# A four-layer graph network on one Trainium2 core: the end of the nearest-neighbour search, the bias, the third pass's row order and the attention loop's first loads are moved

## The chip, the cores and the metric

One core of a Trainium2 chip (trn2) runs the whole kernel. The metric is the device time of one execution in microseconds (us), as the median of several runs, lower is better. The profile shows one execution by its engines: PE (TensorE; PEld is its weight load), DVE (VectorE), ACT (ScalarE), POOL (GpSimd) and SP (SyncE). A name such as SPq is an engine's queue of DMA issues.

## The reference, cut to what matters

The inputs are `x` (2708 nodes of 128 features) and the dense matrix `adj` A (2708 x 2708, f32). Four layers follow each other, each `x = layernorm(x + layer(x))`. Only the first two touch the change:

```python
# layer 0
d  = 1/sqrt(rowsum(A));  z = leaky_relu(d*(A @ (d*x)) @ W1 + b1, 0.1)
S  = exp(-sqrt(max(|z_i - z_j|^2, 0) + 1e-10) / 2), kept for the 4 nearest j of each i
d2 = 1/sqrt(rowsum(A + S))
x  = layernorm(x + d2*((A + S) @ (d2*x)) @ W2 + b2)
# layer 1
XW  = x @ W;  s_col = XW @ a[:128];  s_row = XW @ a[128:]
den = exp(leaky_relu(s_row[:,None] + s_col[None,:], 0.01));  num = A @ den
x   = layernorm(x + A @ ((den/num) @ XW))
# layers 2 and 3: a normalised and a plain product with A, each with a linear map
```

## The kernel before

**Tiles.** The 2708 nodes are T = 22 tiles of 128 rows: 21 full ones and a last one of 20. The 2708 columns are C = 6 chunks (four of 512, one of 384, one of 276), each of three or four tiles. `adjT` holds A transposed in HBM. The tile `ring` takes its strips as they are loaded; `res` keeps the last RES = 6 tiles of rows.

**Stages in order of time.** The first product with A and the projection to `z` end at about 155 us. The search (L699 to L702) then takes one tile of nodes at a time: twelve matmuls give the negated distances, ACT copies them to `key`, and DVE finds the eight largest (`max`, L701) and their places (`max_index`, L702). The order of the tiles is 4 to 15, 0 to 3, 16 to 20; tile 21 was done early. `weigh` turns the four nearest of some tiles into weights (`sim`), the degrees into `d2inv`, and `x` into `y2 = d2inv * x`, which is written to HBM as `y_rows`. It is called for tiles 0 to 16 after tile 16, for 17 to 19 after tile 19, and for 20 and 21 after the search. Inside it, `others` finds which neighbour is the node itself and sorts out the other three. Its steps are on POOL, except for tiles 20 and 21, where DVE does them.

The second pass (L204, `by_panels`) is A times `y2`, chunk by chunk. Meanwhile POOL gathers three neighbours for each tile from `y_rows` (`gather_near`, L729), and DVE sums them with their weights (`sum_near`, L738 and L742). PE, DVE and ACT run in an order written by hand here: an object `Due` counts one tick per row tile of the product, and `at(n, f)` runs `f` at tick n. `near_at[t]` is the tick of `sum_near(t)`. A chunk is closed by `end_pass2`: its neighbour sums are added on PE (`add_near`, L749) at tick `max(due.n + 1, near_at[last tile] + 3, ended[-1] + 16)`, followed by the layer's linear map (L780), the bias and the norm (`norm0`), a transposition (L798) and the comparisons that rank all nodes. The bias `b2` is added to all of `xs` at once (`add_bias`, L265), before the pass.

The third pass (`turns`, L1337) sums weighted rows of A to make the carries of the attention loop. A `line` is half a row tile of A, loaded by SP into one of eleven berths in `ring`, `more` and `y_place` (`load_line`, L1035). As soon as PE has read a berth, the next line that uses it is loaded. An `own_line` is half a tile of `res` and needs no load. `turns` is the order, written by hand, in which PE takes lines, the ranking matmuls (`in_rank_order`, `counts`, `ranks_known`, `in_list_order`) and the weights of the loop (`next_weights`). `end_half(h)` copies the sums of half h out of PSUM and sends them into the tile `carry` by four DMAs on ACT's queue (L1363).

Then comes a branch (`tc.If`, L1773) on a flag which all engines read (L1512), and behind it the attention loop of 44 steps, `block_layer`. In step i, `load(i)` brings the rows by two gathers on POOL (L1498) and two small DMAs on SP (L1505, from `carry`); PE makes `num` (L1619) in a wide and a narrow piece; ACT inverts it (L1452, L1455); DVE corrects and scales it (L1462, L1466, L1469); `keep` saves two rows of the error into `carry` (L1634, four DMAs on SP); and PE adds the product up (L1477). Each step is loaded two steps ahead, into one of three strips of `ring`. The loop's first ACT instruction is the load of a function table (L1609). Layers 2 and 3 follow from about 730 us on.

Every DMA that SP and ACT issue takes the next of eight completion semaphores and waits until the DMA eight before it has ended.

Of the kernel before, what the change touches and what calls it, by code (L numbers as in the profile page):

```python
# [13 lines left out]
ALU = mybir.AluOpType  # L14
# [38 lines left out]
def kernel(  # L53
# [310 lines left out]
    with tc.tile_pool(name="knn", bufs=1) as knn:  # L364
# [225 lines left out]

        def weigh(ts):

            t0, t1 = ts[0], ts[-1] + 1
            nr, sm = near[:, t0:t1, :TOPK], sim[:, t0:t1, :]

            nc.vector.tensor_add(nr, nr, nsq[:, t0:t1, None].to_broadcast([P, t1 - t0, TOPK]))
            nc.vector.tensor_scalar(nr, nr, 0.0, DIST_EPS, op0=ALU.min, op1=ALU.subtract)
            nc.scalar.activation(sm, nr, AF.Ln, scale=-1.0)
            nc.scalar.activation(sm, sm, AF.Exp, scale=0.5)
            nc.scalar.activation(sm, sm, AF.Exp, scale=-0.5)  # L600
            dd = d2inv[:, t0:t1]
            nc.vector.tensor_reduce(dd, sm, AX.X, ALU.add)
            nc.vector.tensor_add(dd, dd, deg[:, t0:t1])  # L603
            nc.scalar.activation(dd, dd, AF.Ln)
            nc.scalar.activation(dd, dd, AF.Exp, scale=-0.5)
            if t1 < T:
                nc.gpsimd.tensor_mul(
                    y2[:, t0:t1, :], xs[:, t0:t1, :], d2inv[:, t0:t1, None].to_broadcast([P, t1 - t0, D])
                )
            else:  # L610
                scale_rows(y2, xs, d2inv, ts)
                spread(y2[:, FULL, :])
# [5 lines left out]
            if full < t1:  # L618
                queue.dma_start(y2_rows[FULL * P :, :], y2[:LAST, FULL, :])
            else:  # L620
                for a in range(t0, t1, 11):
                    others(range(a, min(a + 11, t1)), nc.gpsimd)

# [48 lines left out]
        ready = [load_panel(g, 0) for g in range(G)]  # L672
        tc.keep_in_program_order(nc.scalar.preload_act_table_set("natural_log_exp_and_others"))
        with tc.tile_pool(name="keys", bufs=3) as keys:

            for n, t in enumerate([*range(4, S), *range(4), *range(S, FULL)]):
# [18 lines left out]
                for c in range(C) if n else (5, 3, 2, 4, 1, 0):  # L695
                    if not n:
                        norms(c)
                    cs = cols[c]
                    nc.tensor.matmul(pks[c][:p, : cw[c]], lhsT=z2[:, :p], rhs=zT[:, cs], start=False, stop=True)  # L699
                    nc.scalar.copy(key[:p, cs], pks[c][:p, : cw[c]])  # L700
                nc.vector.max(near[:p, t, :], key[:p])  # L701
                nc.vector.max_index(where[:p, t, :], near[:p, t, :], key[:p])  # L702
                if t == T - 6:
                    weigh(range(0, T - 5))
                if t == T - 3:
                    weigh(range(T - 5, T - 2))
            weigh(range(T - 2, T))
            others(range(T - 2, T), nc.vector)

    psum.close()  # L710
# [62 lines left out]
    nc.vector.memset(rows_d, 0.0)  # L773
    add_bias(b2_sb)
    rk = rk_pool.tile([P, T], F32, tag="rk", name="rk")
# [181 lines left out]
    at = due.at  # L957
    near_at = [24 + (23 * t) // 5 for t in range(T)]
    for t in range(T):
        at(near_at[t], sum_near, t)  # L960
    at(20, nc.vector.memset, rk_f, float(OOB))

# [66 lines left out]
    def line_at(n):  # L1029

        return berths[stays[n]]
# [15 lines left out]
    def fetch_xw(xws, q):  # L1047
# [3 lines left out]
            oob_is_err=False,  # L1051
        )

    with tc.tile_pool(name="rank", bufs=1) as rank:
# [296 lines left out]

        HEADS = 96

        def end_half(h):
# [4 lines left out]
            nc.scalar.copy(tot[:, : edges[4] - edges[3]], banks[h][:, : edges[4] - edges[3]])  # L1359
            nc.scalar.copy(tot[:64, edges[4] - edges[3] :], banks[h][:64, edges[4] - edges[3] : span])  # L1360
            for g in range(4):
                w = edges[g + 1] - edges[g]
                nc.scalar.dma_start(  # L1363
                    carries[0][HEADS : HEADS + 2 * NCH, h * HALF + edges[g] : h * HALF + edges[g + 1]],
                    tot[32 * g : 32 * g + 2 * NCH, :w],
                )
# [45 lines left out]
        def line(n):  # L1412
            for _ in range(n):
                at = loaded[0]
                loaded[0] += 1
                i, h = lines[at]
                add_line(i, h, line_at(at), last=at == 2 * S - 1)
                if at in follows:
                    load_line(follows[at])

        def own_line(n):
            for _ in range(n):
                h, i = divmod(held[0], FULL - S)
                held[0] += 1
                add_line(S + i, h, res[:, i, h * HALF : (h + 1) * HALF], last=held[0] == FULL - S)
                if held[0] == FULL - S:
                    end_half(0)

        turns = [
            (line, 4), (blocks_of_edges,), (line, 7), (own_line, 2), (last_xw,), (in_rank_order, 0), (line, 2),  # L1430
            (in_rank_order, 1), (line, 2), (in_rank_order, 2), (count_lone,), (line, 2), (counts,), (line, 1),
            (add_last_rows, 0), (own_line, 3), (line, 2), (ranks_known,), (line, 1), (own_line, 1), (in_list_order, 0),
            (line, 1), (in_list_order, 1), (in_list_order, 2), (line, 1), (own_line, 1), (in_list_order, 3),
            (line, 1), (add_last_rows, 1), (next_weights,), (own_line, 1), (next_weights,), (line, 1), (next_weights,),
            (own_line, 1), (next_weights,), (line, 1), (next_weights,), (own_line, 1), (line, 1), (next_weights,),
            (line, 5),
        ]
        for f, *args in turns:
            f(*args)
        for c in range(C):  # L1440
            nc.sync.dma_start(res[few(c), FULL - S, cols[c]], adjT[FULL * P :, cols[c]])
        end_half(1)
        carry = carries[0]
        assert loaded[0] == 2 * S and held[0] == 2 * (FULL - S) and work["groups"] == 6
        xws, lw = work["xws"], work["lw"]
        order.close()
    more.close()
# [33 lines left out]
    psum.close()  # L1481
    adj_half = adjT.rearrange("n (h k) -> (n h) k", h=2)
    WIDE = 2 * CW
    NARROW = HALF - WIDE
    assert 0 < NARROW <= CW

    def block(s):

        return s % NCH * CH + s // NCH

    steps = [(h, q) for h in range(2) for q in range(NQ)]
    rows = {}

    def load(i):
        h, q = steps[i]
        rows[i] = strip(i).rearrange("p (n k) -> p n k", n=2)
        for n in range(2):
            nc.gpsimd.indirect_dma_start(  # L1498
                out=rows[i][:KC, n, :], out_offset=None, in_=adj_half[:, :],
                in_offset=bass.IndirectOffsetOnAxis(ap=slot_i[h][:KC, 2 * q + n : 2 * q + n + 1], axis=0),  # L1500
                bounds_check=2 * N - 1, oob_is_err=False,
            )
            b = block(2 * q + n)
            at = 2 * b if b % CH else HEADS + b // CH * 2
            nc.sync.dma_start(rows[i][KC : KC + 2, n, :], carry[at : at + 2, h * HALF : (h + 1) * HALF])  # L1505

# [97 lines left out]
    def block_layer():  # L1604
        with (
# [40 lines left out]
            with tc.manual_schedule(engines={e.engine for e in engines}):  # L1646
                load(0)
                load(1)
                late_q = list(range(SOON, NQ))
# [165 lines left out]
```

## Time and profile before

| what | us |
|---|---|
| median of three runs | 1066.23 (1063.72 to 1070.17) |
| the profiled execution, its own time | 1063.12 |
| its span, first to last instruction | 1061.4 |
| PE busy | 984.6 (93%) |
| DVE / ACT / POOL busy | 637.0 / 331.5 / 275.1 |
| search, last matmul ends | 286.9 |
| second pass, first matmul | 287.46 |
| third pass, first line | 442.42 |
| third pass, last line ends | 499.04 |
| loop, first `num` / first `hacc` | 502.04 / 512.60 |

In a timeline row the columns are start, duration, engine, line, operation, tiles and shapes, count, and in brackets the idle time of that engine just before it and what ended it. A waits row gives who waited for whom: total us, times, longest. A windows row gives the length of a stretch, the busy time of PE, PEld, DVE, ACT and POOL (with counts), the granted PE clock (1.00 is full speed), the busy share of the DMA engines and GB/s. A busy PE is not a PE at its peak: a matmul at half clock is busy for longer.

### The profile page before, as it was taken

What the parts mean: (1) busy time and instruction counts of PE and PEld (TensorE: products, weight loads), DVE (VectorE), ACT (ScalarE), POOL (GpSimd) and SP (SyncE); (2) the same over time, 40 slices, a digit from 0 to 9 for tenths busy, and PEclk for the clock granted to TensorE, in tenths of its full rate; (3) what the DMA queues carried; (4) which work ended last, traced back from release to release, by engine and by line L of the source; (5) the groups of instructions that cost most, each with busy time, mean ns of one, the idle gap of its engine ahead of it and who ended that gap; (6) DMA issues with size and microseconds to landing.
All of it is one profiled execution on the core that took longest, in us unless ns stands there. A gap on an engine that the chain in (4) does not pass through costs nothing.

```text
span 1061.4 us, 11655 instructions
## 1 busy us (share of the span) xinstructions
PE 984.6 (93%) x3773; PEld 482.9 (45%) x3773; DVE 637.0 (60%) x1358; ACT 331.5 (31%) x609; POOL 275.1 (26%) x339
## 2 busy tenths in 40 slices
PE   0898999999998998796899999999999999999996
PEld 0346544444444556562333333334445544564444
DVE  5985438999944577862899999994121121222222
ACT  0000126555501245402767776762010100010000
POOL 4000000000477673023788534430121100000000
PEclk9989999999998998698999999999999999999998
DMA  9999340000185666696455555556665957484652
GB/s 339 373 342 270 109 157 1 0 1 1 32 279 183 221 182 201 224 359 200 118 167 152 149 146 157 142 163 215 219 193 169 308 168 219 145 276 149 227 170 72
DMA packets 102001, 191.00 MB, mean 180 GB/s; under 512 B 14022, under 2 KB 43342, under 8 KB 101930
## 3 DMA queue, kind: packets, MB, share of 16 engines
q1 hardware_dynamic: 83764, 152.22, 43.5%
q0 software_dynamic: 17728, 37.62, 12.8%
q8 instruction: 32, 0.52, 0.2%
q10 hardware_dynamic: 438, 0.31, 0.1%
q14 instruction: 39, 0.32, 0.1%
HBM read 214.80 MB, written 4.16 MB: 206 GB/s over the span
## 4 chain that ended last, share of the span: by engine, by line
PE 48%; DMA 1%; DVE 1%; ACT 1%; issue 1%; POOL 0%; POOLq 0%; DVEq 0%
PE acc L204 28%; PE num L1619 9%; PE hacc L1477 9%; PE mis L285 1%; DMA ring<-carry 1%; DMA ring<-in_adjT,slot_i 0%; PE mis L1750 0%; DVE inv L1466 0%; DVE err L1462 0%; ACT gb L234 0%; PE mis L1716 0%; DVE inv L1469 0%; PE mis L1746 0%; ACT inv L1452 0%; POOL rstd L253 0%
## 5 line engine op out<-in xcount | busy, mean ns | idle before, releaser
L1498 POOL DMA_INDIRECT ring<-in_adjT,slot_i x88 | 104.4, 1187 | 95.9 <-PE num L1619 67.0
L1619 PE MATMUL num<-ring,lw 128*64 128x512 f32 (+1 forms) x528 | 113.7, 557 | 6.1 <-DMA ring<-carry 3.8
L1477 PE MATMUL hacc<-inv,xws 128*128 128x512 f32 (+1 forms) x264 | 111.7, 559 | 0.6 <-ACT inv L1455 0.3
L699 PE MATMUL acc<-zT,z 128*128 128x512 f32 (+2 forms) x252 | 102.2, 552 | 0.0
L1452 ACT ACTIVATE inv<-num,plain 128x1024 f32<-128x1024 f32 x88 | 80.6, 916 | 57.6 <-PE num L1619 41.4
L253 POOL TENSOR_TENSOR rstd<-rstd,minus_half 128x4 f32<-128x4 f32 (+1 forms) x18 | 17.3, 960 | 313.5 <-DVE rstd L252 313.5
L234 ACT COPY gb<-acc 128x512 f32<-128x512 f32 (+2 forms) x18 | 9.6, 535 | 251.1 <-PE acc L204 251.1
L1462 DVE TENSOR_TENSOR err<-inv,num 128x1024 f32<-128x1024 f32 x88 | 74.6, 856 | 21.0 <-ACT inv L1455 19.7
L700 ACT COPY key<-acc 128x512 f32<-128x512 f32 (+2 forms) x126 | 67.1, 535 | 55.1 <-issue 27.9
L204 PE MATMUL acc<-ring,y 128*128 128x512 f32 (+2 forms) x192 | 82.0, 558 | 0.5 <-issue 0.5
L1477 PEld LDWEIGHTS hacc<-inv,xws 128*128 128x128 f32 x264 | 46.5, 189 | 77.6 <-issue 34.2
L729 POOL DMA_INDIRECT got<-y_rows,where x66 | 71.5, 1083 | 26.6 <-DVE near_sum L742 8.9
L204 PE MATMUL acc<-ring,xs 128*128 128x512 f32 (+2 forms) x192 | 78.1, 550 | 0.0
L1469 DVE SCALAR_TENSOR_TENSOR inv<-gb,g_inv,inv 128x1024 f32<-128x1024 f32 x88 | 77.2, 917 | 0.1
L204 PE MATMUL acc<-ring,carry 128*128 128x512 f32 (+2 forms) x192 | 74.5, 542 | 0.0
L204 PE MATMUL acc<-ring,m_rows 128*128 128x512 f32 (+2 forms) x192 | 74.3, 542 | 0.0
L1466 DVE SCALAR_TENSOR_TENSOR inv<-err,inv 128x1024 f32<-128x1024 f32 x88 | 72.3, 861 | 0.1
L575 POOL TENSOR_TENSOR slot_e<-near,sim 128x44 f32<-128x44 f32 (+2 forms) x3 | 0.7, 241 | 267.3 <-DVE d2inv L603 265.2
L699 PEld LDWEIGHTS acc<-zT,z 128*128 128x128 f32 x252 | 45.8, 190 | 50.4 <-issue 45.0
L1455 ACT ACTIVATE inv<-inv 128x1024 f32<-128x1024 f32 x88 | 67.6, 768 | 2.8
L1619 PEld LDWEIGHTS num<-ring,lw 128*64 128x64 f32 x528 | 37.4, 138 | 65.0 <-issue 47.5
L701 DVE MAX8 near<-key 128x8 f32<-128x2708 f32 x21 | 62.3, 2965 | 2.7 <-ACT key L700 2.7
(376 smaller groups left out, 1370.0 us busy)
## 6 DMA issues: line engine op xcount, KB each, us to landing
ring<-in_adjT SPq DMA_DIRECT2D x74, 1024.0 KB
ring<-in_adjT SPq DMA_DIRECT2D x20, 677.0 KB
ring<-in_adjT SPq DMA_DIRECT2D x17, 768.0 KB
part<-in_adjT SPq DMA_DIRECT2D x12, 1024.0 KB
ring<-in_adjT SPq DMA_DIRECT2D x17, 552.0 KB
more<-in_adjT SPq DMA_DIRECT2D x10, 677.0 KB
res<-in_adjT SPq DMA_DIRECT2D x4, 1280.0 KB
part<-in_adjT SPq DMA_DIRECT2D x3, 768.0 KB
```

Of the source, the lines that this page charges most:

```text
L204: nc.tensor.matmul(accs[c][: lhsT.shape[-1], :w], lhsT=lhsT, rhs=src, start=start, stop=stop)
L699: nc.tensor.matmul(pks[c][:p, : cw[c]], lhsT=z2[:, :p], rhs=zT[:, cs], start=False, stop=True)
L700: nc.scalar.copy(key[:p, cs], pks[c][:p, : cw[c]])
L729: nc.gpsimd.indirect_dma_start(out=got[:p, :], out_offset=None, in_=y2_rows[:, :], in_offset=bass.IndirectOffsetOnAxis(ap=where[:p, t, k : ...
L1452: nc.scalar.activation(inv, num[:, :w], AF.Ln, scale=plain[:, 0:1], bias=plain[:, 1:2])
L1455: nc.scalar.activation(inv, inv, AF.Exp, scale=-1.0)
L1462: nc.vector.tensor_mul(err, inv, num[:, :w])
L1466: nc.vector.scalar_tensor_tensor(inv, err, 2.0, inv, op0=ALU.subtract, op1=ALU.mult)
L1469: nc.vector.scalar_tensor_tensor(inv, gb[:, col : col + w], g_inv[:, q : q + 1], inv, op0=ALU.max, op1=ALU.mult)
L1477: nc.tensor.matmul(haccs[:, o:e], lhsT=xws[:, q, :], rhs=inv[:, o:e], start=(q == 0), stop=(q == NQ - 1))
L1498: nc.gpsimd.indirect_dma_start(out=rows[i][:KC, n, :], out_offset=None, in_=adj_half[:, :], in_offset=bass.IndirectOffsetOnAxis(ap=slot_i[ ...
L1619: nc.tensor.matmul(num[n * (BJ + 2) : (n + 1) * (BJ + 2), o:e], lhsT=lw[:, 2 * q + n, :], rhs=rows[i][:, n, c0 + o : c0 + e], start=True, ...
```

## The change

- `weigh` is cut in three. `weigh_near` (the distances to `sim`) now runs right after the `max` of a tile, ahead of its `max_index`; `find_d2` (the sum and the inverse root) and `keep_y2` (`y2` and its write to `y_rows`) follow. For tiles 20 and 21 all of it is done before the `max_index` of tile 20. From the `max` of tile 19 on, DVE runs in the order written. `others` of tiles 0 to 16 now stands behind the write of their `y2` in the source; in the built program POOL has both groups of `others` first, then the multiplication of tiles 0 to 16 and its DMA, then those of tiles 17 to 19, then `others` of 17 to 19.
- The bias is added chunk by chunk at ticks of the second pass (`add_b2`), and `near_at` begins at 20 instead of 24 and rises by 4.8 instead of 4.6.
- In `turns` loaded lines come earlier: 27 instead of 23 of the 32 are behind PE when the last `in_list_order` begins, and the pass ends with the last rows and two own lines instead of five loaded lines.
- `load(0)` and `load(1)` are issued ahead of the branch. The four sends of half 1 go from ACT's queue to SP's, behind those two loads and ahead of the small `res` loads for the next pass.
- The exponentials of `csort` stand ahead of the sends of half 0 on ACT in the built program.

```diff
-        def weigh(ts):
+        def weigh_near(ts):
...
+        def find_d2(ts):
...
+        def keep_y2(ts):
...
-            else:
-                for a in range(t0, t1, 11):
-                    others(range(a, min(a + 11, t1)), nc.gpsimd)
...
+                if t == T - 3:
+                    ends.enter_context(tc.manual_schedule(engines={nc.vector.engine}))
                 nc.vector.max(near[:p, t, :], key[:p])
+                if t == T - 3:
+                    weigh_near(range(T - 5, T - 2))
+                if t == T - 2:
+                    weigh_near(range(T - 2, T))
+                    others(range(T - 5, T - 2), nc.gpsimd)
+                    find_d2(range(T - 2, T))
+                    keep_y2(range(T - 2, T))
                 nc.vector.max_index(where[:p, t, :], near[:p, t, :], key[:p])
+                if t == T - 3:
+                    find_d2(range(T - 5, T - 2))
+                    keep_y2(range(T - 5, T - 2))
                 if t == T - 6:
-                    weigh(range(0, T - 5))
-                if t == T - 3:
-                    weigh(range(T - 5, T - 2))
-            weigh(range(T - 2, T))
+                    weigh_near(range(0, T - 5))
+                    find_d2(range(0, T - 5))
+                    keep_y2(range(0, T - 5))
+                    for a in range(0, T - 5, 11):
+                        others(range(a, min(a + 11, T - 5)), nc.gpsimd)
             others(range(T - 2, T), nc.vector)
...
-    add_bias(b2_sb)
...
-    near_at = [24 + (23 * t) // 5 for t in range(T)]
+    near_at = [20 + (24 * t) // 5 for t in range(T)]
+
+    def add_b2(ts):
+        rows = xs[:, ts[0] : ts[-1] + 1, :]
+        nc.vector.tensor_add(rows, rows, b2_sb[:, None, :].to_broadcast([P, len(ts), D]))
+
+    for ts in chunk_tiles:
+        at(near_at[ts[0]], add_b2, ts)
...
+            if h == 0:
+                send_half(h, tot, nc.scalar)
+
+        def send_half(h, tot, queue):
+
             for g in range(4):
...
         turns = [
-            (line, 4), (blocks_of_edges,), (line, 7), (own_line, 2), (last_xw,), (in_rank_order, 0), (line, 2),
...
-            (line, 5),
+            (line, 4), (blocks_of_edges,), (line, 7), (last_xw,), (in_rank_order, 0), (line, 3),
+            (in_rank_order, 1), (line, 3), (in_rank_order, 2), (count_lone,), (line, 2), (counts,), (line, 3),
+            (add_last_rows, 0), (own_line, 4), (ranks_known,), (line, 2), (own_line, 1), (in_list_order, 0),
+            (line, 1), (in_list_order, 1), (in_list_order, 2), (line, 2), (in_list_order, 3),
+            (next_weights,), (own_line, 1), (next_weights,), (line, 2), (next_weights,),
             (own_line, 1), (next_weights,), (line, 1), (next_weights,), (own_line, 1), (line, 1), (next_weights,),
+            (line, 1), (add_last_rows, 1), (own_line, 2),
         ]
...
-        for c in range(C):
-            nc.sync.dma_start(res[few(c), FULL - S, cols[c]], adjT[FULL * P :, cols[c]])
         end_half(1)
...
+        load(0)
+        load(1)
+        send_half(1, heads[:, span:], nc.sync)
+        for c in range(C):
+            nc.sync.dma_start(res[few(c), FULL - S, cols[c]], adjT[FULL * P :, cols[c]])
...
             with tc.manual_schedule(engines={e.engine for e in engines}):
-                load(0)
-                load(1)
```

## The prediction

> **What bounds the kernel now.** PE is busy for 984.6 of 1061.4 us, so time can only come from the places where PE waits or runs at a low clock. I read first what PE waited for, longest first; then PE's own timeline around the two largest waits; then the queues that feed it there; then the clock and the DMA load in windows.
>
> ```profile
> PE acc L749 <- DVE near_sum L742: 4.6, 1, 4.6
> PE num L1619 <- DMA ring<-carry: 3.8, 2, 3.0
> PE acc L1337 <- DMA ring<-in_adjT: 3.7, 1, 3.7
> PE mis L852 <- ACT xT L801: 2.6, 1, 2.6
> PE acc L1337 <- SPq L1811: 2.3, 1, 2.3
> PE num L1619 <- DVE err L1462: 1.8, 1, 1.8
> ```
>
> Apart from the start of the kernel (29.2 us on the degree sums, untouched), these are all its large waits, and five of the six lie where the diff cuts: the first chunk's neighbour sums, the last lines of the third pass, and the first steps of the loop.
>
> ```profile
> 320.56 0.97 PE L749 MATMUL acc<-ident,near_sum 128*128 128x128 f32 x6
> 326.13 0.80 PE L749 MATMUL acc<-ident,near_sum 128*128 128x128 f32 x2 [4.60 <-DVE near_sum L742]
> 326.73 3.62 PE L204 MATMUL acc<-res,y 128*128 128x512 f32 x4
> 330.14 1.55 PE L780 MATMUL mis<-w,hT 128*128 128x128 f32 x8
> ...
> 494.48 0.90 PE L1337 MATMUL acc<-ring,lc 128*32 128x339 f32 x8 [3.71 <-DMA ring<-in_adjT]
> 497.69 1.35 PE L1337 MATMUL acc<-more,lc 128*32 128x339 f32 x8 [2.31 <-SPq L1811]
> 502.04 5.94 PE L1619 MATMUL num<-ring,lw 128*64 128x512 f32 x20 [3.00 <-DMA ring<-carry]
> 509.81 2.50 PE L1619 MATMUL num<-ring,lw 128*64 128x330 f32 x12 [1.83 <-DVE err L1462]
> ```
>
> See the durations behind each wait: four L204 matmuls take 3.62 us after the first wait and 1.88 elsewhere, a line takes 1.35 instead of 0.75. A wait costs more than its own length.
>
> ```profile
> 282.61 3.82 POOL L607 TENSOR_TENSOR y<-xs,d2inv 128x2176 f32<-128x2176 f32 x1
> 298.53 3.08 POOL L585 CAST where<-near 128x9 uint32<-128x9 f32 x1
> 305.34 1.15 POOL L729 DMA_INDIRECT got<-y_rows,where  x1 [2.41 <-DMA y_rows<-y]
> ...
> 480.57 1.00 POOL L1048 DMA_INDIRECT xws<-xw_rows,row_j  x1 [0.30 <-issue]
> 481.88 1.07 POOL L1498 DMA_INDIRECT ring<-in_adjT,slot_i  x1 [0.30 <-issue]
> ...
> 497.74 6.61 SPq L1505 DMA_DIRECT2D ring<-carry  x6
> 499.64 3.23 ACTq L1363 DMA_DIRECT2D carry<-heads  x4
> 503.88 1.28 ACT L1609 ACT_TABLE_LOAD   x1 [4.27 <-SPq L1811]
> ```
>
> ```profile
> 413.00:416.00 3.00, 2.02 (x4) 1.29 (x5) 0.12 (x1) 1.26 (x4) 0.00 (x0) 0.51 0.53 216
> ...
> 480.00:486.00 6.00, 6.00 (x62) 2.48 (x64) 4.28 (x11) 2.46 (x8) 4.63 (x5) 1.00 0.46 101
> 486.00:495.00 9.00, 5.29 (x63) 1.94 (x62) 3.54 (x9) 2.46 (x8) 2.09 (x2) 1.00 1.00 305
> ```
>
> The DMA engines are half idle at 480 to 486 us and full right after: lines and the loop's gathers are asked for late and together. SP's first small load at 497.74 coincides with the last line's landing (PE resumes at 497.69): by its completion slot it had to wait for that line.
>
> **Part 1, search and bias: 5.5 us gained.** Before, the last `y_rows` write was issued at 301.55 to 302.40. It stood behind a cast on POOL that took 3.08 us instead of about 0.2, as long as the 3.09 us bias add ran on DVE (298.46 to 301.55); the first gather came at 305.34. After: the last `max` ends near 292.3 (291.04, plus 1.3 for the small DVE steps now between the scans: eight at 0.15 to 0.2). Two DVE steps, three ACT steps, two DVE, two ACT and the 0.45 us multiply take 2.4 us, as at 294.16 to 296.86 before. ACT's two writes go out by 295.9; landing took 2.9 us (302.40 to 305.34); first gather about 298.8, so 6.5 earlier. PE now asks for the first sums 3 ticks of 0.86 us = 2.6 sooner. Twelve gathers at 1.31 us follow one another, so tile 3's sum moves with the first gather, from 326.1 to 319.6, and PE, from the shift below, wants it near 319.7. The wait goes. Its price by the rows: 320.56 to 331.52 is 10.96 us for work that takes 3.5 at full clock (0.90 + 1.72 + 0.89, rows at 348 to 352 us): 7.45 us.
>
> Against it: POOL now does both `others` groups before the 3.82 us multiply that PE's pass needs. They can begin when the `sim` values are there, near 276.1 (ACT's last exponential behind tile 18's copies at 275.4), and take 8.5 us by their rows (3.45 + 0.3 + 0.95 + 3.8). The multiply ends at 288.4 instead of 286.43, and PE starts at 288.5 instead of 287.46: 1.05 lost. Nothing covers that. The scan (`max_index`) of tile 20 ends near 297.7 instead of 294.1. That is covered: its places are read by the last gathers, which went out around 400 us. If it weren't, 3.6 us. The bias add by chunks is six of about 0.45 to 0.6 us. Four lie where DVE idles; the last two stand in its full stretch 399 to 412 us ahead of the L852 wait: 0.4 lost. One batch of seventeen ranking matmuls now stands ahead of the last L749: 0.55 lost. PE's order else only shifts. Sum: 7.45 - 1.05 - 0.95 = 5.45.
>
> **Part 2, the third pass: 6.9 gained.** 32 lines, 10 own lines and the rest are all still computed; only the order changes. From 490.78 PE needs 1.35 us for its last two lines and took until 499.04, 8.26: 6.9 are waiting and half clock. A line is 0.69 MB and takes 1.67 us at the 408 GB/s measured at 447 to 471. With 27 lines read before the last list step, the berth of line 29 is free near 476 (PE's row times summed in the new order), and lines 30 and 31 near 480, instead of 484.21 to 488.64. They land by 486, also against the gathers, and are read at 487 to 490. The list step itself comes two lines, 1.6 us, later, and POOL's ranking output one: the gathers move from 481.88 to 483.2 and land by 493, when `num` begins. If lines 30 and 31 still come behind two gathers (1.7 us each), up to 3.4 of the 6.9 are lost.
>
> **Part 3, the loop's start: 3.0 gained.** Let E be the end of the third pass on PE. Before, `num` began at E + 3.0, when the small loads landed, ACT's first inverse at E + 6.7 (second small load, table load) and the second `hacc` at 518.88 = E + 19.84. After, the small loads of steps 0 and 1 lie behind the last line and land long before E. The gathers gain nothing by standing ahead of the branch: POOL passed it in the usual 0.30 us (480.57 to 481.88) and was held by six fetches of 1.31. ACT, without its 3.23 us of sends, has its table by about E + 2.6 (copies 0.6, the 1.0 seen between its last send and the table load, 1.28), and `num` lets it start then. First `hacc`: E + 2.6 + 6.86 (505.74 to 512.60) = E + 9.4. But SP now has queued ahead of step 2's small loads: four sends that wait for ACT's copies (E + 0.6), 0.6 to 0.78 each, three `res` loads in 1.34, the flag, the branch. I take 1.0 for the branch, as on ACT. The load goes out at E + 5.4 and, landing in 4.4 (497.74 to 502.04, 512.00 to 516.5), arrives at E + 9.8 where `num` wants it at E + 7.9. Second `hacc`: E + 16.8. Gain 3.0, out of 4.4 without this new wait.
>
> [...] The 2.65 us wait at 411.3 halved the clock from 413.5 to 419.5, and the 4.60 us wait left it at 0.50 until 5.2 us after PE resumed. [...] by the row they may halve the clock for 5 us, 2.5 lost. [...] for the gaps zero is likelier, since 1.83 at 508 left the clock at 1.00, and 2.5 goes into the range. [...] POOL's row shows 0.30, ACT's 1.0; between zero and SP's 7.4 hidden before (490.36 to 497.74) I keep 1.0.
>
> **Sum.** 5.5 + 6.9 + 3.0 = 15.4. Against the profiled execution, 1063.1 gives 1047.7; the median of the runs is 3.1 higher, 1066.2 gives 1050.8. I predict 1050.5.
>
> **Rivals.**
> A (0.65), the sum above: 1047 to 1054.
> B (0.20), the loop's start gives nothing: SP's branch or the halved clock eats the 3.0, perhaps with some late lines. For it: ACT's 1.0, the 2.65 row. Against: POOL's 0.30. Gain 9 to 12: 1054 to 1057.
> C (0.09), the gathers start no earlier: the write of `y_rows` now lands among the panel loads, with DMA full at 291 to 300 us. PE then resumes at 326.1 as before, but 3 ticks less far: part 1 loses 2.6 + 0.95 = 3.5 instead of gaining 5.5: 1059.8. Against it: before, the last writes landed in 2.9 us with DMA at 0.83 busy.
> D (0.03), slower: the loop becomes bound by SP. It issues six small DMAs of 0.56 to 0.61 us per step of 4.89, each behind the completion of the eighth before it. The new order gives them other slots; if each step were held by 0.47 us more, 44 steps would cost 20.7, 5.3 more than the 15.4 gained: 1071.5. From 0.35 us per step on there is no gain. Against it: 3.6 us of issue per 4.89 leaves room, and the slots still pass in turn.
> E (0.03), more gained: SP's landing is shorter and the tail's L852 wait shrinks: 1045. That parts 1 or 2 do not do what they say is unlikely, since the built order shows them moved.
>
> **The numbers.** 0.5% is 5.3 us, about what a measurement of this kernel can tell from no change. Range 1044 to 1059: A, B and E with the spread of the runs (2.5 below and 3.9 above their median), leaving out C and D. Faster by over 0.5%: A, B, E and half of C, which lies near the bound, 0.93; within 0.5%: the rest of C, 0.04; slower: D, 0.03.
>
> **What would show it.** Right: no wait of L749 on `near_sum`; PE's second pass starting 1.6 us after the search's last matmul, not 0.53; no wait of L1337 on a line; PE clock 1.00 through the third pass; first `num` within 1 us of the last own line; a wait of about 2 us on step 2's small load. Wrong: a multiply L615 ending after 289.5; a first gather after 301; a line landing after 490; PE idle for more than 9 us in the first 20 us of the loop.

## The result and the profile after

The changed kernel takes 1055.78 us (five runs, 1054.56 to 1063.47) against 1066.23 us before: 0.990 of it, with a 95% interval of 0.987 to 0.993. That is 10.5 us gained where the sum of the prediction had 15.4. The first profiled execution of the changed kernel is the 1063.47 us one; it had the PE clock at half speed for 20.5 us in the third pass, so the changed kernel was run and profiled once more, unedited (`again`: 1055.27 us, 0.9916 of the kernel before, interval 0.988 to 0.995; its profiled execution took 1057.01). The lines below are from that second profile unless the text says otherwise.

Waits of PE in `again` (total us, times, longest), to be set beside the six of before (that of L871 is unchanged at 2.6 and left out):

```profile
PE num L1653 <- DVE err L1517: 5.1, 1, 5.1
PE acc L769 <- DVE near_sum L762: 3.0, 1, 3.0
PE acc L204 <- POOL y L615: 1.6, 1, 1.6
PE num L1653 <- ACT heads L1407: 0.7, 1, 0.7
```

The waits for lines (3.7 and 2.3) and for the loop's first small loads (3.8) are gone. The wait on `near_sum`, which the prediction took away, is still there, and the loop's start has a new one of 5.1 on `err`.

Durations by stage show where the time came from. They are differences of timeline rows, so a shift of the whole profile drops out:

| stretch | before | `again` | change | foretold |
|---|---|---|---|---|
| last search matmul to second pass's start | 0.53 | 1.61 | +1.1 | +1.05 |
| second pass's start to third pass's first line | 154.96 | 151.64 | -3.3 | -6.5 |
| third pass | 56.62 | 51.97 | -4.7 | -6.9 |
| end of third pass, E, to the second `hacc` | 19.84 | 19.36 | -0.5 | -3.0 |
| second `hacc` to the last of the loop | 204.89 | 202.90 | -2.0 | 0 |

These sum to 9.4 us. The two spans differ by 6.1, since outside the stretches `again` happens to be 3.3 longer (1.8 up to the search's end, 1.5 behind the loop). Single executions differ in the second row too: six with part 1 and the sums at its ticks have 151.6 to 154.2, three without it 153.8 to 155.0. Timeline rows of `again` around the first chunk's sums:

```profile
286.46 3.82 POOL L615 TENSOR_TENSOR y<-xs,d2inv 128x2176 f32<-128x2176 f32 x1
286.90 3.40 DVE L596 TENSOR_TENSOR sim<-near,nsq 128x12 f32<-128x12 f32 x1
290.33 10.57 PE L204 MATMUL acc<-ring,y 128*128 128x512 f32 x24 [1.61 <-POOL y L615]
305.06 1.18 POOL L749 DMA_INDIRECT got<-y_rows,where  x1 [4.50 <-DMA y_rows<-y]
324.76 0.49 PE L769 MATMUL acc<-ident,near_sum 128*128 128x128 f32 x2 [3.04 <-DVE near_sum L762]
325.08 2.90 PE L204 MATMUL acc<-ring,y 128*128 128x512 f32 x4
```

An addition of 12 columns, 0.15 us before, took 3.40: it ends 0.02 us after POOL's multiply. The last `max` is late behind it. The writes of `y_rows` then took 4.95 us to land, from the end of the last issue on ACT at 300.11 to the gather at 305.06, not 2.9. The DMA engines were full from 300 to 305 us (90% busy or more in every quarter of a microsecond, against a mean share of 0.62 in the kernel before).

Rows of `again` at the end of the third pass and the start of the loop:

```profile
492.60 1.34 PE L1386 MATMUL acc<-res,lc 128*32 128x339 f32 x16
494.53 3.64 SPq L1415 DMA_DIRECT2D carry<-heads  x4
494.61 4.31 PE L1653 MATMUL num<-ring,lw 128*64 128x512 f32 x20 [0.66 <-ACT heads L1407]
499.95 1.20 ACT L1507 ACTIVATE inv<-num,plain 128x1024 f32<-128x1024 f32 x1 [4.00 <-DMA res<-in_adjT]
500.65 1.42 SPq L1101 DMA_DIRECT2D ring<-carry  x2
504.02 3.81 PE L1653 MATMUL num<-ring,lw 128*64 128x330 f32 x12 [5.11 <-DVE err L1517]
507.76 2.54 PE L1532 MATMUL hacc<-inv,xws 128*128 128x512 f32 x6
```

`num` begins 0.67 us after E = 493.94 and ACT's table is loaded by E + 2.0 (495.95), both as foretold. But ACT's first inverse starts only at E + 6.0, and PE stands still for 5.1 us behind it. The twelve `num` matmuls after that wait take 3.81 instead of 2.50: half clock.

### The profile page after: what moved, and what is told of

Read it like the earlier page. It is cut to its first block, busy times and chain, and to the rows that moved or that the text cites. A ratio compares the mean times of both kernels' runs of the same rounds, so it can differ in the third digit from the quotient of the medians.

```text
span 1061.7 us, 11661 instructions
## 1 busy us (share of the span) xinstructions
PE 989.3 (93%) x3773; PEld 485.6 (46%) x3773; DVE 641.6 (60%) x1363; ACT 332.4 (31%) x609; POOL 261.0 (25%) x339
## 4 chain that ended last, share of the span: by engine, by line
PE 49%; DVE 1%; ACT 1%; issue 0%; POOL 0%; POOLq 0%; DVEq 0%
PE acc L204 28%; PE hacc L1532 10%; PE num L1653 9%; PE mis L285 1%; PE mis L1782 0%; DVE inv L1521 0%; DVE err L1517 0%; ACT gb L234 0%; PE mis L1748 0%; DVE inv L1524 0%; PE mis L1778 0%; POOL rstd L253 0%; PE mis L1736 0%; ACT m_rows L160 0%; DVE xs L277 0%
## 5 line engine op out<-in xcount | busy, mean ns | idle before, releaser
L1094 POOL DMA_INDIRECT ring<-in_adjT,slot_i x88 | 93.0, 1057 | 96.6 <-PE num L1653 77.8
L204 PE MATMUL acc<-ring,y 128*128 128x512 f32 (+2 forms) x192 | 83.6, 565 | 1.6 <-POOL y L615 1.6
L204 PE MATMUL acc<-ring,xs 128*128 128x512 f32 (+2 forms) x192 | 77.8, 549 | 0.0
L204 PE MATMUL acc<-ring,carry 128*128 128x512 f32 (+2 forms) x192 | 74.5, 542 | 0.0
L204 PE MATMUL acc<-ring,m_rows 128*128 128x512 f32 (+2 forms) x192 | 74.3, 542 | 0.0
L705 PEld LDWEIGHTS acc<-zT,z 128*128 128x128 f32 x252 | 45.8, 190 | 50.4 <-issue 45.0
```

The source lines that it names most:

```text
L204: nc.tensor.matmul(accs[c][: lhsT.shape[-1], :w], lhsT=lhsT, rhs=src, start=start, stop=stop)
L1094: nc.gpsimd.indirect_dma_start(out=rows[i][:KC, n, :], out_offset=None, in_=adj_half[:, :], in_offset=bass.IndirectOffsetOnAxis(ap=slot_i[ ...
```

## The experiments

The kernels below ran in four groups, each on a chip of its own: `again` and the three parts; `heads_kept`, `mul4`, `later6` and `dinv_late`; `xw_split`, `load2` and `best3`; and `best4`. The kernel before, run beside each group, had medians of 1065.5, 1065.6, 1083.6 and 1081.9 us. Times are therefore compared by their ratio to the kernel before on the same chip, with the 95% interval in brackets. Edits are cut to the lines that matter. Each kernel but the changed one was profiled once, so a difference between two profiles can be scatter where no other run bears it out.

### The change again, and its parts alone

`again` is the changed kernel itself.

> The whole change once more, unedited. Of its five times one was 1063.5 us and four 1054.6 to 1055.8, and the profiled execution is the 1063.5 one: its PE clock was 0.50 from 453.9 to 475 us, in the middle of the third pass, after a stretch (451 to 453.3 us) in which PE was busy for 2.96 of 4 us. Theory: that half clock is an accident of one execution and is the whole distance between the two groups. Then a second profiled execution shows clock 1.00 from 444 to 500 us, the first num some 8 to 10 us earlier (about 493 to 494) and a time of about 1055. Rival: the half clock is in every execution of this order. Then it shows again, num begins at 502 to 503 again, and the distance between the times has another source.

Measured: 1055.27 us. Half clock came again, but for 6.8 us; from 459 us on it was 1.00 (windows of `again`; the third to last number is the granted clock):

```profile
446.00:452.00 6.00, 4.96 (x55) 2.26 (x47) 5.83 (x14) 1.14 (x6) 0.97 (x2) 1.00 1.02 413
452.00:457.00 5.00, 5.00 (x32) 3.14 (x35) 4.83 (x13) 0.15 (x1) 0.74 (x2) 0.51 1.02 412
```

So both sides were half right: the fall is in every profile of this order, and its length differs. In the 1063.47 us execution the third pass took 58.45 us instead of 51.97, which is as much as the two executions differ (1063.47 and 1057.01).

Added up over windows, the half clock in the third pass lasted 3.4 us in four of the eight profiles that have this order and not the edit of `xw_split` below, 6.8 in two, 10.2 in one and 20.5 in one. Why one fall lasts 3.4 us and another 20.5 stays open; in the longest, PE was busy throughout.

`p1_only` is part 1 on the kernel before: `weigh` cut in three, the bias by chunks and the new `near_at`, and nothing else of the change.

> Part 1 alone (search split, bias by chunks, neighbour sums due earlier) on the kernel before. By the record's sum 5.45 us gained: about 1060.8 against 1066.2. Theory from the changed kernel's trace: the 4.4 us wait of PE on near_sum is still there (DVE's 12-column addition took 3.41 us beside POOL's 3.82 us multiply, the second y_rows writes took 4.8 us to land, the first gather came at 303.9), the pass starts 1.05 later, the tail has 0.95 more, while the gathers come 1.4 earlier: between 2 us lost and 1 us gained, within 0.3% of the kernel before.

Measured: 1064.76 us, 0.998 (0.996 to 1.001): 0.7 us, not told from nothing. In its profiled execution (1075.28 us, the slowest of its fourteen, with half clock for 17 us of the third pass) DVE's addition took 3.44 us and PE waited 3.9 us on `near_sum`.

`p2_only`, part 2 on the kernel before:

```diff
- (line, 4), (blocks_of_edges,), (line, 7), (own_line, 2), (last_xw,), ... (line, 5),
+ (line, 4), (blocks_of_edges,), (line, 7), (last_xw,), ... (add_last_rows, 1), (own_line, 2),
```

> Part 2 alone (the order of the third pass: loaded lines first, the last two own lines at the end) on the kernel before. By the record's sum 6.9 us gained: about 1059.3. Theory from the traces: the waits for lines (3.7 and 2.3 us) and the half clock behind them are gone, 7 to 8 us gained. Rival: the lines of the last turns are replaced by a wait of PE for the loop's small loads, which still stand behind the branch and, by their completion slot, behind the last lines: then num begins at the end of the pass + 3.0 as before, and the gain is still 7, since that wait was there before. If the gain is under 5, the waits for lines were shorter than they looked, or the gathers now collide with lines.

Measured: 1059.4 us, 0.994 (0.992 to 0.996): 6.1 us gained. No wait on a line is left; `num` waits 3.3 us for the small load, as the rival said (its waits row; two waits, the longest 3.3):

```profile
PE num L1619 <- DMA ring<-carry: 3.8, 2, 3.3
```

`p3_only`, part 3 on the kernel before:

```diff
+        load(0); load(1); send_half(1, heads[:, span:], nc.sync)   # ahead of the branch, res loads behind them
-                load(0); load(1)                                   # in the loop
```

> Part 3 alone (the loop's first two loads ahead of the branch, the second half's four sends on SP behind them) on the kernel before, whose third pass keeps its own order. By the record's sum 3.0 us gained: about 1063.2. Theory from the changed kernel's trace: ACT's first inverse waits until all four sends on SP have landed (5.3 us after the pass's end) because it writes memory that they read from; first hacc at the pass's end + 13.8 instead of + 13.6 before, second at + 18.7 instead of + 19.8: 1 us gained, up to 3 if the kernel before also loses 1.9 us at 531 to 538 us by a gather that this order avoids. In this kernel the small loads of steps 0 and 1 stand behind the last lines on SP, so num may start later than 0.7 us after the pass.

Measured: 1062.26 us, 0.995 (0.993 to 0.998): 3.2 us gained. The three parts add up to 10.0; the whole change gave 10.2. Each of these is known to within 2 to 4 us only, so that they fit so closely is in part luck.

### Where the loop's 2 us come from: one POOL instruction

In the kernel before, POOL's power `dinv` for the next layer stands among the loop's gathers. In the changed kernel the built program has it in front of step 3's gathers. First the rows of before, then of the changed kernel's first profile:

```profile
526.49 4.02 POOL L253 TENSOR_TENSOR dinv<-dinv,minus_half 128x22 f32<-128x22 f32 x1
530.74 1.75 POOL L1498 DMA_INDIRECT ring<-in_adjT,slot_i  x1 [0.22 <-PE hacc L1477]
538.09 1.93 PE L1619 MATMUL num<-ring,lw 128*64 128x512 f32 x6 [0.43 <-DMA ring<-in_adjT,slot_i]
```

```profile
502.90 3.90 POOL L253 TENSOR_TENSOR dinv<-dinv,minus_half 128x22 f32<-128x22 f32 x1
507.01 1.09 POOL L1094 DMA_INDIRECT ring<-in_adjT,slot_i  x1 [0.21 <-PE num L1653]
```

`dinv_late` puts it back:

```diff
+    def dinv_power():
+        nc.gpsimd.tensor_tensor(dinv, dinv, minus_half[:, :T], op=ALU.pow)
...
+                    if i == 4:
+                        dinv_power()
```

> The changed kernel with one instruction put back where the kernel before has it: POOL's power dinv (3.9 to 4.0 us) stands among the loop's gathers, behind step 6's, instead of in POOL's idle time before step 3's. Theory: part 3 gains little at the loop's start and the rest because this power no longer delays the gathers: from the second hacc to the loop's last one the kernel before and the two with loads behind the branch took 204.9, 207.6 and 205.9 us, with waits of num on a gather at 530 to 560 us, and the three with the loads ahead 203.1, 202.9 and 202.9. Then here it is 204.5 to 206 again, with such waits, POOL's gathers taking 1.2 to 1.3 us on average over 500 to 600 us instead of 1.1: 2 to 3 us slower than the changed kernel, 1057 to 1058. Rival: what keeps the gathers on time is the other order at the loop's start (first two loads, fetches), not the power's place: 203 us stays.

Measured: 1059.41 us, 0.994 (0.992 to 0.996), and from the second `hacc` to the last one 205.81 us (513.96 to 719.77) instead of 202.90. POOL's gathers average 1.19 us over 500 to 600 us instead of 1.13. So the loop of this profile is 2.9 us longer, as the theory said. The other profiles outside the last two groups agree: the stretch took 204.9 to 207.6 us in the four with the power among the gathers (this one included) and 202.9 to 203.1 in the six with the power ahead of step 3's. The whole times alone (0.994 against 0.992) do not tell the two apart. Three gathers of 1.04 to 1.21 us, their gaps of 0.3 and about 1 us of waiting fill a step of 4.9, so POOL can make up 4 us only over several steps.

### The first chunk's sums

`mul4` cuts POOL's multiply:

```diff
-                nc.gpsimd.tensor_mul(y2[:, t0:t1, :], xs[:, t0:t1, :], ...)
+                for a in range(t0, t1, 5):
+                    nc.gpsimd.tensor_mul(y2[:, a:b, :], xs[:, a:b, :], ...)      # b = min(a + 5, t1)
```

> The changed kernel with POOL's multiply of tiles 0 to 16 in four pieces (three of 5 tiles, one of 2; about 1.1 us each) instead of one of 3.82 us. Theory: DVE's two-input addition of 12 columns took 3.4 us because it can't run beside a POOL elementwise instruction and waits for the end of that instruction. Then with pieces it takes at most about 1.2 us, the last max ends 2.2 us earlier, the first gather comes about 2 us earlier and PE's wait on near_sum shrinks from 3.0 to 4.4 us to 1 to 2.4; 2 to 4 us less than the changed kernel. Rival one: DVE can't get in between pieces either (the next piece begins at once): 3.4 us stays. Rival two: the addition is quick, but the gathers stay, since the landing of the y_rows writes among the panel loads takes the time back: no gain.

Measured: 1054.91 us, 0.992 (0.988 to 0.995), no gain to be told. DVE's rows in `mul4`:

```profile
286.79 0.78 DVE L596 TENSOR_TENSOR sim<-near,nsq 128x12 f32<-128x12 f32 x1
287.61 1.18 DVE L597 TENSOR_SCALAR sim<-sim 128x12 f32<-128x12 f32 x1
```

DVE got in between the pieces (the four took 4.26 us), so its wait here is one for the running POOL instruction. PE's wait for the multiply fell from 1.6 to 0.5 us. The first gather came 15.0 us after the last search matmul instead of 16.3, but PE still waited 4.3 us on `near_sum`. So the second rival was right that nothing is gained, but the time was lost in a later landing than the one that it named. The twelfth gather, the last that these sums need, also went out 1.0 us sooner, but its data were summed 4.9 us after its end instead of 3.8, and so no earlier (at 324.40; 324.35 in `again`). The first profile of the changed kernel has 4.9 there too, so this landing varies from one execution to the next.

`later6` leaves the gathers as they are and asks for the sums later:

```diff
-        n = max(due.n + 1, near_at[chunk_tiles[c][-1]] + 3, ended[-1] + 16)
-        ended.append(n)
+        n = max(due.n + 1, near_at[chunk_tiles[c][-1]] + (3 if c else 9), ended[-1] + 16)
+        ended.append(n if c else n - 6)
```

> The changed kernel with the first chunk's neighbour sums (the four L769 matmuls and what follows them in that chunk) asked for six steps of the pass later, 5.2 us at 0.86 each; the other chunks keep their places. Theory: PE's wait of 3.0 to 4.4 us on near_sum and the half clock after it are only a matter of where PE asks; the part's gain of 7.45 us that the record counted on is there, but not by an earlier gather. Then no wait of L769 over 0.5 us, clock 1.00 through 320 to 335 us, and 4 to 7 us less than the changed kernel: about 1049 to 1051. Rival: the work of that chunk now runs into the next one's (transposes, copies, ranking), and a new wait of 1 us or more appears before 345 us; or the sums of the second chunk come too late in turn.

Measured: 1049.76 us, 0.986 (0.983 to 0.989), 5.5 us less than `again` and 5.1 less than `heads_kept` and `mul4` on its own chip. The wait is gone and the four L204 behind it run at full clock; the stretch from the second pass's start to the third pass's first line took 148.06 us instead of 151.64:

```profile
325.45 1.05 PE L769 MATMUL acc<-ident,near_sum 128*128 128x128 f32 x8
326.34 1.88 PE L204 MATMUL acc<-res,y 128*128 128x512 f32 x4
```

No new wait appears before 345 us. The gain that the prediction counted on existed, and it needed no gather earlier than the changed kernel's. The delay alone, without part 1, was not run.

### The loop's start

In the built program ACT's first inverse waits for the end of SP's four sends of the heads, since the tile `inv` takes over their memory. (The row above names another DMA of SP, issued right behind them, as the releaser.) `heads_kept` puts the heads elsewhere:

```diff
+        m_row = row_tile("m_rows")
         end_half(1)
-            tot = heads[:, h * span : (h + 1) * span]
+            tot = heads[:, :span] if h == 0 else m_row[:, :span]
```

> The changed kernel with one edit: the second half's heads lie in a tile that the loop first writes after its 22nd step, instead of memory that the loop's first inverse reuses. Theory: in the changed kernel ACT's first inverse waited (3.4 us) for SP's four sends of the heads to land, DVE's err behind it, and PE 4.5 to 5.1 us behind both, with half clock after it. Then here ACT's first inverse starts at the third pass's end E + 2.6 (4.0 at most) instead of E + 5.4, PE's wait on err is 2.5 us or less and the clock stays at 1.00, first hacc by E + 10 instead of E + 13.8, and the second by E + 17 instead of E + 18.7 to 19.4, where step 2's small load (issued at E + 6.2) bounds it: about 2 us less than the changed kernel, 1053. Rival: ACT waits for something else (the res loads on SP, the branch): nothing moves.

Measured: 1054.85 us, 0.991 (0.988 to 0.994). ACT came on time (E = 496.29, so E + 2.8), but PE met the next late thing (ACT's row, PE's, and a window of PE's clock, in `heads_kept`; PE's wait on `err` fell to 1.88):

```profile
499.07 1.20 ACT L1508 ACTIVATE inv<-num,plain 128x1024 f32<-128x1024 f32 x1 [0.77 <-DMA carry<-m_rows]
505.18 1.76 PE L1654 MATMUL num<-ring,lw 128*64 128x512 f32 x2 [1.27 <-DMA ring<-carry]
506.00:508.00 2.00, 1.66 (x4) 0.33 (x4) 2.00 (x4) 0.00 (x0) 1.70 (x2) 0.50 0.45 125
```

The first `hacc` came at E + 13.6. The cause of ACT's wait is shown; my expectation of E + 10 was wrong, because step 2's `num` stands ahead of the first `hacc` on PE and its small load, issued at E + 6.4, was not there. Nor did the clock stay at 1.00, as I had expected and as the expectation of `load2` below still says: it was 0.50 for 3.4 us from about 505 us on, after PE's waits of 1.88 and 1.27 us.

`load2` is `heads_kept` with that load moved ahead too:

```diff
         load(1)
+        load(2)
         send_half(1, m_row[:, :span], nc.sync)
```

> The changed kernel with the heads kept in memory that the loop's first inverse does not reuse, and with step 2's gathers and small loads ahead of the branch too (before SP's four sends of the heads). With the heads moved alone, ACT's first inverse came at E + 2.8 and the clock stayed at 1.00, but PE then waited 1.3 and 0.3 us for step 2's small load (issued at E + 6.4, used at E + 11), and the first hacc stayed at E + 13.6. Theory: that small load is the second bound at the loop's start. Then here the wait on the small load is gone, the first hacc comes at E + 9.5 to 10.5, the second at E + 14.5 to 16 instead of E + 18.5, and the time is 3 us less than with the heads moved alone: about 1052. Rival: PE is then held by DVE's err or by the gathers of step 3, which stand behind POOL's power dinv of 3.9 us: 1 us or less.

Measured: 0.993 (0.990 to 0.996). With E = 514.34 the start is as expected:

```profile
521.18 2.50 PE L1655 MATMUL num<-ring,lw 128*64 128x330 f32 x12 [1.88 <-DVE err L1519]
524.02 2.51 PE L1534 MATMUL hacc<-inv,xws 128*128 128x512 f32 x6 [0.34 <-issue]
```

First `hacc` at E + 9.7, second at E + 14.7: 4.7 us sooner than in `again`. Its waits of 1.88 and 0.34 us left the clock at 1.00. But the loop from there on took 205.07 us. The power (516.55 to 520.45) now stands in front of gathers that are wanted sooner, which is the likely reason; `best4` tests it. Nothing of the sooner start shows in the time.

### The clock in the third pass

`xw_split` groups the last tiles' transposes:

```diff
-(line, 7), (last_xw,), (in_rank_order, 0)        # transpose, copy, matmul, three times
+(line, 6), (last_xT,), (line, 1), (last_xw,), (in_rank_order, 0)   # 3 transposes, a line, 3 matmuls
```

> The changed kernel with the last tiles' three transposes of the third pass in one group, one line behind them, and their three matmuls after that line, instead of transpose, wait for ACT's copy, matmul, three times in a row (PE idle for 0.35, 0.41 and 0.27 us within 3 us). In all seven executions seen with the new order of the third pass, PE's clock fell to 0.50 some 1 us after that stretch (at 450 to 457 us) and stayed there for 5 to 21 us; with the order of before it did so in one of three. Theory: the idle spots bring the fall, now that no two own lines stand ahead of them. Then here the clock is 1.00 from 446 to 490 us, the three groups on val_q take 1.53 us each and the lines between them 1.9, and the third pass is about 3 us shorter: 1052. Rival: the clock falls for another cause (DMA at full load from 448 us on, the 44-column groups on val_q themselves): it falls all the same, at the groups on val_q, and nothing is gained.

Measured: 0.991 (0.988 to 0.994), not told from `again`. The clock did what the theory said; the window behind the stretch, in `xw_split`:

```profile
466.00:475.00 9.00, 9.00 (x98) 5.43 (x98) 8.76 (x20) 0.16 (x1) 0.83 (x2) 1.00 1.01 411
```

All eight profiled executions that have the new order without this edit show the fall, `load2` on the chip of `xw_split` and `best3` among them; the three with it (`xw_split`, `best3`, `best4`) do not. In the order of before, with two own lines ahead of the same idle spots, one of three does (`p1_only`). The third pass took 50.1, 52.1 and 50.4 us in the three with the edit. In the eight without it, it took 51.1 to 52.0 in five, 53.8 and 54.1 in `later6` and `load2`, and 58.45 in the first profile. So some 2 us of part 2's gain may have gone there, more when the fall is long; the times do not show it.

### All together

`best3` joins `later6`, `mul4`, `load2` and `xw_split`; `best4` also moves the power into the third pass:

```diff
-        inv_sqrt_of(dinv, deg, DEG_EPS)          # after the loop's code
+(count_lone,), (dinv_power,), (line, 2)          # same two instructions, in POOL's and DVE's idle time
```

> All edits together on the changed kernel: first chunk's sums asked for six steps later, POOL's multiply in four pieces, the last tiles' transposes in one group, the heads in other memory, step 2's loads ahead of the branch. If they add up: 5.5 (sums later, measured) + 1.1 (PE's pass starts without its wait for the multiply) + 3 + 3.5 = 13 less than the changed kernel, about 1042. If the clock falls in the third pass all the same and the small load was not the bound, 1048.

> All edits together as before, and POOL's power dinv moved out of the loop: between the count of the lone columns and the counts of the third pass, where POOL is idle from 454 to 474 us and DVE from 461 to 467. With step 2's loads ahead the second hacc came at E + 14.1 to 14.7, as expected, but the loop from there to its last hacc took 205.1 and 207.9 us instead of 202.9, with waits and POOL's gathers at 1.2 us on average: what the start gained went back into the loop. Theory: it is again the power, 3.9 us on POOL in front of step 3's gathers, which the earlier loop now meets. Then without it the loop takes 203 us again, the gathers 1.1 us on average, and the time is 3 to 5 us under the version without this edit: 0.980 to 0.982 of the kernel before. Rival: POOL has no slack for a start so early, with three gathers of 1.3 us per step of 4.9 and DVE beside it: 205 us or more stays, and the ratio stays at 0.985.

Measured: 0.985 (0.981 to 0.989) and 0.985 (0.982 to 0.988). Both lie below the change as it stands (0.990 and 0.992), with intervals that just overlap, and neither is told from `later6` alone (0.986). In `best3` the loop from the second `hacc` took 207.88 us, in `best4` 204.15, and in that only one step was late (1.2 us, at 576.6). So moving the power may have helped the loop, but `xw_split`, where the power was not moved, has 204.48, and the start of `best4` was slower (second `hacc` at E + 16.2 instead of E + 14.7, the clock at half for 3.4 us). The ratio stayed at 0.985, as the rival said, and the sum of 13 us that I had expected is not there.

Something else was in the way on these chips. In all four kernels run there, ACT did not start the copy `hT<-acc` (L999, or L1001) when its input was ready, and PE waited for it: 14.2 and 3.3 us in `load2`, 15.2 in `best3`, 9.1 and 4.4 in `xw_split`, 4.5 in `best4`. The profile gives no releaser in this case (`remote` or `issue`). It would account for much of the 16 to 18 us by which the kernel before was slower there, but that kernel was not profiled on these chips. What holds ACT stays open, and so does what the smaller edits would give without it.

## Why the prediction was right or wrong

The forecast of 1050.5 was 5 us low; 1055.8 lies inside the stated range and is the time given for rival B (the loop's start gives nothing, 1054 to 1057), but not for B's reason: the missing 5 us are part 1's. A loop's start that gives next to nothing, as B says, came true as well, and a gain further on in the loop made up for it. That was luck: the prediction put the rest of the loop at nothing. Of its own signs, the start of the second pass (1.61 us), the lines without waits and the first `num` came as said; the wait on `near_sum` stayed, the clock fell in the third pass, the wait on step 2's small load did not show, and the first gather came after 301, a sign of being wrong. Step by step:

- **Part 1, 5.45 foretold, 0.7 measured.** The step that failed is "first gather about 298.8, so 6.5 earlier". Counted from the last search matmul it is 11.9 us foretold, 16.3 in `again`, 18.4 before: 2.1 gained, 4.4 missing. Of these 2.4 are the last write's issue (11.4 instead of 9.0), late with the last `max` by DVE's addition behind POOL's multiply, and 2.0 the landing, with the DMA engines full; that the panel loads made it longer fits this and was not tested alone. I had seen that the order of the build puts the multiply behind `others`, and priced it for PE only (1.05, measured 1.1). I did not ask which DVE instruction would run beside it. The row for that was in my own list: POOL's cast of 3.08 us beside DVE's bias add of 3.09. An estimate from it, with the longer instruction now on POOL, has the addition last as long as the rest of the multiply of 3.82 us, which is 3.4; by the row of before it costs 0.15. The trace gave 3.40, and with the multiply in pieces 0.78. Rival C named the landing among the panel loads, and that was about half of it. "Tile 3's sum moves with the first gather" did not hold to the microsecond either: with a gather 1.3 us earlier, `mul4` summed no sooner.
- **The wait's own price was right.** 7.45 us for the wait and its half clock, less 0.95 for the tail, make 6.5. The stretch lost 3.3 in `again` and another 3.6 in `later6`, together 6.9, from one profile each.
- **Part 2, 6.9 foretold, 6.1 measured.** All waits for lines went. What I had wrong is the sign "PE clock 1.00 through the third pass": with the two own lines gone from ahead of them, idle spots of 0.36, 0.41 and 0.27 us brought half clock in eight profiles of eight, and without the spots in none of three. (A line of 0.69 MB at 408 GB/s takes 1.70 us, not 1.67; nothing rests on it.)
- **Part 3, 3.0 foretold, 3.2 measured, for another reason.** `num` at E + 0.7 and the table at E + 2.0 were right. The failed step is "`num` lets it start then": ACT's inverse came at E + 6.0, since it overwrites what SP's sends read. I had moved the four sends from ACT to SP and counted what they delay on SP, not who waits for their end. The foretold wait on step 2's small load is real, but it was hidden behind this one and came out in `heads_kept`. The start gave 0.5 in `again`, 1.1 in the first profile and 1.6 in `p3_only`. The rest, 2 us in `again` and 2.9 by `dinv_late`, is the place of the power `dinv`, an instruction that the diff does not name.
- **The clock and the branch.** The half clock that I left in the range for PE's gaps at the loop's start came, with a gap of 5.1 us instead of 2.4, and cost 1.3 us (3.81 instead of 2.50) where I had put 2.5. With gaps near those foretold, of 2.4 and 1.9, it came in `heads_kept` (1.88 and 1.27, with 0.78 of work between) and not in `load2` (1.88 and 0.34): "zero is likelier" held in one profile of the two. Of the branch: SP's small load went out 1.2 us after the last `res` issue (499.47 to 500.65), near the 1.0 that I had taken.
- **Rival D** can be closed: the steady steps of `again` take 4.89 us, with SP's new order of slots too.

## What to carry to other kernels

When an instruction is moved, also ask three things of the built program: what runs beside it on another engine (3.40 us instead of 0.15 for an addition here), who waits for the end of a transfer that is moved (also whoever takes over its memory), and which instructions without an edit moved past a full queue. When an engine waits for a result, compare the price of bringing the result earlier with that of asking for it later: on the changed kernel six steps of delay gave 5.5 us, while the edits upstream had given 0.7. And an idle spot is to be priced with the clock behind it: three of a third of a microsecond were followed by 3.4 to 20.5 us at half clock.

## What the runs showed of the hardware that was not expected

- A short DVE operation took 3.40 us beside a POOL multiply of 3.82, and it ended with it; cut in four, 0.78 and then 1.18 for the one-input operation behind it (0.17 in `again`). In the kernel before, DVE's `max` and `max_index` ran beside the same multiply and took their usual 2.96 and 2.98 us.
- Half clock came after gaps far shorter than any wait that I had priced: 1.04 us idle in 6, in three pieces. In the third passes of nine profiles it lasted 3.4, 6.8, 10.2, 17.0 or 20.5 us.
- POOL's gathers took 1.04 to 1.21 us each in the steady loop of `again` and up to 2.06 in the kernel before (a mean of 1.31 over 500 to 600 us). What lengthens them was not tested.
- On two chips PE waited 3.3 to 15.2 us at a time in the second pass for an ACT copy whose input was there, for a reason that the profile does not show.
